# Sparse graph attention on one core: sums of products on DVE for more tiles, an earlier request of h, and record loads from another queue

## The chip, the cores and the metric

The kernel runs on one core of a Trainium2 chip. The metric is the device time of the program in microseconds; lower is better. A core has these engines: TensorE (PE, with its weight load PEld), VectorE (DVE), ScalarE (ACT), GpSimd (POOL) and SyncE (SP). Each runs its own instructions in a fixed order, and they wait for one another through semaphores. DMAs are issued by SP, ACT and POOL; those of one engine stand in that engine's order like its other instructions.

## The reference

One layer of graph attention with a residual, for 4096 nodes with 512 features, 8 heads of 64. Cut to what matters:

```python
hs = layer_norm(x, ln1_scale, ln1_bias)           # sources
ht = layer_norm(h_target, ln1_scale, ln1_bias)    # targets
q = (ht @ Wq + bq).reshape(T, H, HD) / sqrt(HD)
k = (hs @ Wk + bk).reshape(S, H, HD)
v = (hs @ Wv + bv).reshape(S, H, HD)
logits = einsum('thd,shd->hts', q, k)
logits = where(adj[None] != 0, logits, -1e30)
ctx = einsum('hts,shd->thd', softmax(logits), v).reshape(T, D)
ht = layer_norm(ht + ctx @ Wo + bo, ln2_scale, ln2_bias)
x = _layernorm(x + ht + gelu(ht @ W1) @ W2)
```

`adj` is 4096 x 4096 and sparse: each entry is set with probability 0.00195, then mirrored, and the diagonal is set, so a target has some 17 sources. All masks are ones. W1 is 512 x 2048, W2 is 2048 x 512. All is float32.

## The kernel before

The kernel has a sparse path, which is the one that runs here, and a dense one behind a flag. The sparse path has these stages.

1. **Projections and lists** (to about 300 us). k and v of all 4096 sources are computed and stored as rows of 1024 numbers in the DRAM table `kvd`. At the same time the rows of `adj` are loaded, and for each target a list of its sources is made; the loads stand in SP's queue. The first 2048 targets are part A, the others part B. In each part the targets are sorted by their number of sources, and a record for each (its count, its own number, its mean and scale for the first norm, its list of sources) is scattered to the table `recs_d`. The lists of part B are made while the first tiles of part A are worked on; the last of them are stored at about 606 us.
2. **Attention**, in 32 tiles of 128 targets. A tile has a fixed number of slots, as many as its longest list may have. In the order of work the tiles, counted from 0, have 11, 13, 14, 15, 15, 16, 17, 17, 18, 19, 19, 20, 22, 23, 24, 39 slots (part A, `NA` = 16 tiles), then 12, 38, 13, 24, 14, 23, 15, 22, 15, 20, 16, 19, 17, 18, 17, 18 (part B). Tile 0 is a group of its own, then tiles 1 and 2, 3 and 4, and so on make groups of two, and tile 31 is one of its own. The ninth tile is tile 8.
3. **Feed-forward** of each group of two tiles (`feed`), woven into the attention of the groups after it.

`_weave` puts attention, feed-forward, the rest of the lists and the loads of weights into one program by costs that are written out in the code. What one engine runs in which order is then settled when the program is built: a scheduling layer orders the instructions of each engine by what they depend on and by the order in which the code issued them. So an instruction that the code issues earlier need not stand earlier on its engine.

**A tile's work.** The record is loaded by `prefetch(i)` (L965 to L979) into one of 7 buffers `rec`; the load of tile i's record therefore waits until the last reader of the record of tile i-7 is done, and that is the scatter of its result to the output (L1281, at the end of `feed`). Tiles 0 and 1 are loaded through POOL's queue, the others through SP's. `front(i)` (L981) then makes q for the tile: POOL gathers the rows of h by the record (`gather`, L964) into a buffer `tq` of 3; ACT normalizes them (L990); PE transposes (L994); ACT scales (L997); PE multiplies by Wq (L1003); DVE adds the bias (L1008). Between these steps stands a `yield`, and every call of `advance` in the attention, two for each slot group, moves each open front one step.

**A slot group** has three slots of a tile (`S` = 3; the last group of a tile may have fewer). For each slot POOL gathers 128 rows of k and v from `kvd`, one for each target (L964, tile `kv`), into a ring of 17 places in part A and 20 in part B. DVE multiplies k by q (L1197) and reduces to logits (L1201). ACT takes exp (L1205 and L1214, and L1178 for the third slot). The weights multiply v: of a full group DVE does the first two slots (L1161) and ACT the third, head by head (`by_scalar`, L1181). PE then transposes the products, four blocks of 128 x 128 a slot, and sums them over the slots of a tile in PSUM (`cps`, L1169). In tiles of part B, DVE first adds the product of the second slot to that of the first (L1165), and PE transposes the sum alone; `values` holds both.

**Order of requests.** `request(k)` asks for slot groups up to four ahead of k in part A and five in part B. `issue(k)`, at the first slot group of tile i, calls `prefetch(i + 2)` and, where tile i has no front yet, starts `front(i)`, so that its gather of h is issued; then it gathers the slots. `finish(i)` is the tail of a tile: it divides by the sum, adds `tq`'s second half (the transposed normalized h, L1092) to the product with Wo (L1096), and so is the last reader of the buffer `tq`; then it takes the second norm.

**The queues around the change.** POOL's queue has all gathers (of kv, h, x), the scatters of results (L1281), the scatters of records (L853) and small powers for the norms (L687). SP's queue has the loads of `adj` (L713), the stores of lists (L766) and the record loads (L978).

Of the kernel before, what the change touches and what calls it, by code (L numbers as in the profile page):

```python
# [17 lines left out]
P = 128  # L18
# [360 lines left out]
RW = E0 + RE  # L379
# [64 lines left out]
def adj_resnorm_kernel(  # L444
# [33 lines left out]
    nc = tc.nc  # L478
# [22 lines left out]
    NA, NBT = len(CAPS_A), len(CAPS_B)  # L501
# [31 lines left out]
    with tc.tile_pool(name="keep", bufs=1) as keep:  # L533
# [17 lines left out]
        with ExitStack() as late:  # L551
# [416 lines left out]
            def prefetch(i):  # L968
                if i >= NT or i in recs:
                    return  # L970
                r0 = TILES[i][0]
                part = 1 if r0 >= PARTS[1][0] * P else 0
                assert part in done
                r0 -= PARTS[part][0] * P
                rec = sp.tile([P, E0 + MAXE], I32, name="rec", bufs=7)

                eng = nc.gpsimd if i < 2 else nc.sync
                eng.dma_start(rec[:, :RW], recs_d[part][r0:r0 + P, :])  # L978
                recs[i] = rec  # L979

            def front(i):  # L981


                rec = recs[i]
                tq = sp.tile([P, 2 * D], F32, name="tq", bufs=3)
                t = tq[:, :D]
                gather(t, h_target, rec[:, TGT:TGT + 1])
                yield
                m = rec[:, RST:RST + 2].bitcast(F32)
                nc.scalar.activation(t, t, AF.Identity, bias=m[:, 1:2], scale=m[:, 0:1])  # L990
                yield
                pt = ps.tile([P, KC, P], F32, name="t", bufs=2)
                for kc in range(KC):
                    nc.tensor.transpose(pt[:, kc, :], t[:, kc * P:(kc + 1) * P], ident)  # L994
                hT = tq[:, D:].rearrange("p (c t) -> p c t", c=KC)
                for kc in range(KC):
                    nc.scalar.activation(hT[:, kc, :], pt[:, kc, :], AF.Identity,  # L997
                                         bias=b1r[:, kc:kc + 1], scale=s1c[:, kc:kc + 1])
                yield
                yield  # L1000
                pq = ps.tile([P, D], F32, name="t", bufs=2)
                for kc in range(KC):
                    nc.tensor.matmul(pq, hT[:, kc, :], wq[:, kc, :], start=kc == 0,  # L1003
                                     stop=kc == KC - 1)
                yield
                yield
                yield
                nc.vector.scalar_tensor_tensor(tq[:, :D], pq, HD ** -0.5, bqr,  # L1008
                                               op0=ALU.mult, op1=ALU.add)
                tqs[i] = tq  # L1010


            SG = [(i, j0, min(S, cap - j0)) for i, (_, cap) in enumerate(TILES)
                  for j0 in range(0, cap, S)]
# [2 lines left out]
            for i, _, n in SG:  # L1017
                if place[-1] + n > RING[i >= NA]:
                    place[-1] = 0
                place.append(place[-1] + n)  # L1020
            first_b = next(k for k, (i, _, _) in enumerate(SG) if i >= NA)
            issued = [0]

            def step(gens, i):

                if i in gens and next(gens[i], StopIteration) is StopIteration:
                    del gens[i]

            def request(k):
# [3 lines left out]
                while issued[0] <= min(k + ahead, len(SG) - 1):  # L1033
# [3 lines left out]
                        assert not mine & set(range(place[m], place[m] + SG[m][2]))  # L1037
                    issued[0] += 1

            def issue(k):  # L1040

                i, j0, n = SG[k]
                if j0 == 0:
                    prefetch(i + 2)
                    if i not in tqs:
                        fronts[i] = front(i)
                        step(fronts, i)
                    if TILES[i][1] > RE:
                        rests[i] = rest_of(i)
                        next(rests[i])  # L1050
                elif j0 + n > 12 and i in rests:
                    for _ in rests.pop(i):
                        pass
                kvs[k] = ring[:, place[k]:place[k] + n, :]
                for j in range(n):
                    gather(kvs[k][:, j, :], kvd[0:N + 1, :], recs[i][:, E0 + j0 + j:E0 + j0 + j + 1])

            def finish(i, p, cps, group, hs, mv):


                rec, tq, cap = recs[i], tqs.pop(i), TILES[i][1]

                nc.vector.scalar_tensor_tensor(p[:, :cap, :], rec[:, E0:E0 + cap].unsqueeze(2)
                                               .to_broadcast([P, cap, H]), 0.0, p[:, :cap, :],
                                               op0=ALU.is_gt, op1=ALU.mult)
                nc.vector.tensor_reduce(sums[:, i, :], p[:, :cap, :].rearrange("p j h -> p h j"),
                                        AX.X, ALU.add)
                ri = sp.tile([P, H], F32, name="ri")
                nc.vector.tensor_scalar_max(ri, sums[:, i, :], SUM_LO)
                nc.vector.reciprocal(ri, ri)  # L1070
                rx = sp.tile([P, KC, P], F32, name="rb", bufs=1)
                rxf = rx.rearrange("p c t -> p (c t)")
                nc.scalar.copy(rxf.rearrange("p (h d) -> p h d", h=H),
                               ri.unsqueeze(2).to_broadcast([P, H, HD]))
                yield
                yield
                prx = ps.tile([P, KC, P], F32, name="t", bufs=2)
                for c in range(KC):
                    nc.tensor.transpose(prx[:, c, :], rxf[:, c * P:(c + 1) * P], ident)
                ct = sp.tile([P, KC, P], F32, name="rb", bufs=1)  # L1080
                nc.scalar.copy(ct, prx)
                yield
                yield
                nc.vector.tensor_mul(ct, cps, ct)
                yield
                yield
                yield
                yield
                pa = ps.tile([P, D], F32, name="t", bufs=2)

                for c in range(KC):
                    nc.tensor.matmul(pa[:, c * P:(c + 1) * P], tq[:, D + c * P:D + (c + 1) * P],  # L1092
                                     ident, is_transpose=True, start=c == 0, stop=False,
                                     skip_group_check=True)
                for c in range(KC):
                    nc.tensor.matmul(pa, ct[:, c, :], wo[:, c, :], start=False,  # L1096
                                     stop=c == KC - 1, skip_group_check=True)
                yield
                h = sp.tile([P, D], F32, name="h")
                nc.scalar.copy(h, pa)  # L1100
                yield
                stats(sp, h, mv[:, len(hs), :], "n2")
                hs.append(h)
                if len(hs) < len(group):
                    return
                nh = len(hs)
                ve = shifted(sp, mv[:, :nh, :], nh, "n2")
                yield
                rs = power(sp, mv[:, :nh, :], nh, "n2", ve)
                yield  # L1110
                nm = negmean(sp, mv[:, :nh, :], rs, nh, "n2")
                for j, h in enumerate(hs):
                    nc.scalar.activation(h, h, AF.Identity, bias=nm[:, j:j + 1], scale=rs[:, j:j + 1])
                yield
                yield
                w = len(hs) * P
                h2T = sp.tile([P, KC, 2 * P], F32, name="h2T")
                for k2 in range(KC // 2):
                    pt = ps.tile([P, 2, 2 * P], F32, name="t", bufs=2)
                    for k in range(2):  # L1120
                        for j, h in enumerate(hs):
                            nc.tensor.transpose(pt[:, k, j * P:(j + 1) * P],
                                                h[:, (k2 * 2 + k) * P:(k2 * 2 + k + 1) * P], ident)
                    for k in range(2):
                        kc = k2 * 2 + k
                        nc.scalar.activation(h2T[:, kc, :w], pt[:, k, :w], AF.Identity,
                                             bias=b2c[:, kc:kc + 1], scale=s2c[:, kc:kc + 1])
                h2Ts[GROUPS.index(group)] = h2T
# [15 lines left out]
            def attention():  # L1144
# [10 lines left out]
                def values(i, j0, n, kv, p, cps, after):  # L1155
# [5 lines left out]
                    nc.vector.tensor_tensor(v4, v4, p[:, j0:j0 + m, :].unsqueeze(3)  # L1161
                                            .to_broadcast([P, m, H, HD]), ALU.mult)
                    slots = list(range(n))
                    if m > 1 and i >= NA:
                        nc.vector.tensor_add(kv[:, 0, D:], kv[:, 0, D:], kv[:, 1, D:])  # L1165
                        slots.remove(1)
                    for j in slots:
# [17 lines left out]
                k = 0  # L1185
# [170 lines left out]
                for g in gens:  # L1356
                    yield from g

            EARLY = 2
            WAIT = 40.0  # L1360
            AHEAD = 4
            UNIT = 60.0
# [102 lines left out]
```

## Time and profile before

| | us |
|---|---|
| median of 4 runs | 1864.02 |
| lowest and highest of them | 1860.98 and 1871.27 |
| the profiled execution | 1860.27 |
| its span, from first to last instruction | 1858.5 |
| granted clock of TensorE, mean | 0.957 |

The costliest groups around the change, with columns line, engine, operation, tiles, shape and count, then the busy time, the mean of one in ns, and the engine's idle time before them with what ended it:

```profile
L964 POOL DMA_INDIRECT kv<-kvd,rec x603 | 757.2, 1256 | 391.4 <-PE cps L1169 154.6 <-issue 134.3 <-DVE kv L1165 55.7
L1169 PE MATMUL cps<-ident,kv 128*128 128x128 f32 x2008 | 265.6, 281 | 48.3 <-DMA kv<-kvd,rec 26.1 <-DVE kv L1161 19.9 <-DVE kv L1165 2.0
L1161 DVE TENSOR_TENSOR kv<-kv,p 128x1024 f32<-128x1024 f32 x202 | 245.6, 1219 | 21.0 <-ACT p L1205 8.3 <-ACT p L1214 7.2 <-issue 3.3
L1165 DVE TENSOR_TENSOR kv<-kv 128x512 f32<-128x512 f32 x101 | 68.8, 686 | 0.3
L990 ACT ACTIVATE tq<-tq,rec 128x512 f32<-128x512 f32 x32 | 26.0, 813 | 112.8 <-DMA tq<-in_L_gnn_h_target_dram,rec 112.4 <-issue 0.4
```

The 603 slots make 2412 transposes; 101 adds save four each, which leaves the 2008 of the second row. Matmuls are pipelined, so the mean of one in the table is longer than the distance between two starts.

### The profile page before, as it was taken

To read this page: it belongs to the slowest core of one execution; us is meant where nothing else is said; L and a number is where in the kernel's file an instruction comes from. 1 tells how busy PE (TensorE), PEld (TensorE's weight loads), DVE (VectorE), ACT (ScalarE), POOL (GpSimd) and SP (SyncE) were. 2 spreads that over 40 slices of the span, in tenths; PEclk is the share of its full clock that TensorE was granted. 3 is DMA by queue.
4 is the path that set the end of the run, shared out by engine and by line. 5 is a ranking of instruction groups with operands and counts; after the bars stand their busy time and mean duration, and the time that the engine had idled before them with its cause. 6 is when DMAs were issued, how large, how long until landed. Compare 5 with 4: busy or idle time off the path is not lost. (4 is left out here: it accounts for less than half of the span.)

```text
span 1858.5 us, 22978 instructions
## 1 busy us (share of the span) xinstructions
PE 1691.9 (91%) x7030; PEld 1105.1 (59%) x7030; DVE 1429.4 (77%) x2596; ACT 1211.3 (65%) x3111; POOL 970.1 (52%) x804
## 2 busy tenths in 40 slices
PE   7989874698989989999998988899999999999995
PEld 3444432475656656767676656566666666656663
DVE  6999855999989838777968998888978798878000
ACT  5767634577877637676767877676868677766211
POOL 1000143846645577657568777776567676652101
PEclk9999987798989999999999999899999999999998
DMA  9999959988877648767778888778777777763000
GB/s 351 366 380 372 344 167 345 340 282 317 285 277 240 207 119 308 259 229 264 251 263 308 279 286 289 236 265 265 225 249 236 241 258 232 251 219 115 23 0 25
DMA packets 147757, 463.28 MB, mean 249 GB/s; under 512 B 24468, under 2 KB 29160, under 8 KB 147624
## 3 DMA queue, kind: packets, MB, share of 16 engines
q0 software_dynamic: 95696, 342.19, 54.2%
q1 hardware_dynamic: 44112, 96.44, 14.6%
q10 hardware_dynamic: 7816, 23.08, 3.2%
q8 instruction: 58, 0.95, 0.2%
q14 instruction: 75, 0.61, 0.1%
HBM read 430.76 MB, written 30.89 MB: 248 GB/s over the span
## 5 line engine op out<-in xcount | busy, mean ns | idle before, releaser
L964 POOL DMA_INDIRECT kv<-kvd,rec x603 | 757.2, 1256 | 391.4 <-PE cps L1169 154.6
L1313 PE MATMUL po<-w,gt 128*128 128x512 f32 x1024 | 468.0, 600 | 7.8 <-ACT gt L1307 7.8
L1304 PE MATMUL pf<-h2T,w 128*128 128x256 f32 (+1 forms) x2176 | 469.4, 370 | 0.0
L1197 DVE TENSOR_TENSOR kv<-kv,tq 128x1536 f32<-128x1536 f32 (+2 forms) x211 | 352.6, 1678 | 111.2 <-DMA kv<-kvd,rec 99.9
L1304 PEld LDWEIGHTS pf<-h2T,w 128*128 128x128 f32 x2176 | 392.2, 192 | 67.0 <-issue 21.8
L1181 ACT ACTIVATE kv<-kv,pa 128x64 f32<-128x64 f32 x1520 | 391.4, 336 | 4.5
L1201 DVE TENSOR_REDUCE lg<-kv 128x24 f32<-128x1536 f32 (+2 forms) x211 | 350.9, 1670 | 6.8 <-ACT pa L1178 5.7
L1313 PEld LDWEIGHTS po<-w,gt 128*128 128x128 f32 x1024 | 189.8, 193 | 205.3 <-issue 196.2
L1169 PE MATMUL cps<-ident,kv 128*128 128x128 f32 x2008 | 265.6, 281 | 48.3 <-DMA kv<-kvd,rec 26.1
L1169 PEld LDWEIGHTS cps<-ident,kv 128*128 128x128 f32 x2008 | 240.8, 146 | 114.8 <-DVE kv L1161 53.5
L1161 DVE TENSOR_TENSOR kv<-kv,p 128x1024 f32<-128x1024 f32 (+1 forms) x211 | 251.4, 1196 | 21.6 <-ACT p L1205 8.8
L687 POOL TENSOR_TENSOR n_rs<-n_ve,mhalf 128x2 f32<-128x2 f32 (+2 forms) x51 | 54.9, 1077 | 356.1 <-DVE n_ve L680 158.8
L728 ACT ACTIVATE kv<-kv 128x1024 uint8<-128x1024 int32 x128 | 134.7, 1053 | 79.6 <-DMA kv<-in_adj_dram 37.4
L1307 ACT ACTIVATE gt<-pf 128x512 f32<-128x512 f32 x128 | 76.3, 596 | 94.0 <-PE pf L1304 88.5
L929 PE MATMUL pq<-wk,h2T 128*128 128x512 f32 x256 | 126.3, 637 | 12.3 <-ACT h2T L914 6.4
L735 DVE MAX8 cand<-kv 128x8 uint16<-128x103 uint16 (+1 forms) x640 | 131.6, 259 | 0.5
L1003 PE MATMUL t<-wq,tq 128*128 128x512 f32 x256 | 119.5, 609 | 10.8 <-ACT tq L997 10.8
L1307 ACT ACT_TABLE_LOAD x99 | 127.0, 1283 | 1.6
L1205 ACT ACTIVATE p<-lg 128x24 f32<-128x24 f32 (+2 forms) x179 | 39.1, 218 | 133.8 <-DVE lg L1201 83.8
L929 PE MATMUL pq<-wv,h2T 128*128 128x512 f32 x256 | 115.3, 593 | 1.0 <-ACT tq L931 1.0
L1096 PE MATMUL t<-wo,rb 128*128 128x512 f32 x256 | 116.1, 595 | 0.0
L990 ACT ACTIVATE tq<-tq,rec 128x512 f32<-128x512 f32 x32 | 26.0, 813 | 112.8 <-DMA tq<-in_L_gnn_h_target_dram,rec 112.4
(156 smaller groups left out, 1582.9 us busy)
## 6 DMA issues: line engine op xcount, KB each, us to landing
kv<-in_adj_dram SPq DMA_DIRECT2D x128, 512.0 KB
kvd<-tq ACTq DMA_DIRECT2D x24, 512.0 KB
kv<-kvd,rec POOLq DMA_INDIRECT x603
kv<-in_L_gnn_h_target_dram SPq DMA_DIRECT2D x32, 256.0 KB
kv<-in_x_dram SPq DMA_DIRECT2D x15, 512.0 KB
rest_d<-gid SPq DMA_DIRECT2D x32, 160.0 KB
w<-in_L_gnn_W_dram SPq DMA_DIRECT2D x4, 1024.0 KB
kvd<-kv ACTq DMA_DIRECT2D x8, 512.0 KB
```

What stands on the lines that cost most here:

```text
L728: nc.scalar.activation(sg, a, AF.Sign, accum_out=dpart[:, i, h:h + 1])
L735: nc.vector.max(cand[:, h * SQ + s, :], wd[:, w0:w1])
L929: nc.tensor.matmul(pkv, hT[:, kc, j * P:(j + 1) * P], w[:, kc, :], start=kc == 0, stop=kc == KC - 1)
L964: nc.gpsimd.indirect_dma_start(out=dst, out_offset=None, in_=table[:, :], in_offset=bass.IndirectOffsetOnAxis(ap=idx, axis=0))
L1161: nc.vector.tensor_tensor(v4, v4, p[:, j0:j0 + m, :].unsqueeze(3) .to_broadcast([P, m, H, HD]), ALU.mult)
L1169: nc.tensor.matmul(cps[:, c, :], kv[:, j, D + c * P:D + (c + 1) * P], ident, is_transpose=True, start=j0 + j == 0 and c == 0, stop=j0 + n ...
L1181: nc.scalar.mul(v, v, pa[:, hd:hd + 1])
L1197: nc.vector.tensor_tensor(kv[:, :n, :D], kv[:, :n, :D], tq[:, :D].unsqueeze(1).to_broadcast([P, n, D]), ALU.mult)
L1201: nc.vector.tensor_reduce(lg[:, :n, :], kv[:, :n, :D].rearrange("p j (h d) -> p j h d", h=H), AX.X, ALU.add)
L1304: nc.tensor.matmul(pf[:, k, :], w1[(f0 + k) // KC][:, kc, (f0 + k) % KC * P:((f0 + k) % KC + 1) * P], h2T[:, kc, :w], start=kc == 0, stop= ...
L1307: nc.scalar.activation(gt, pf, AF.Gelu_apprx_tanh)
L1313: nc.tensor.matmul(po[j], gt[:, k, j * P:(j + 1) * P], w2[(f0 + k) // KC][:, (f0 + k) % KC, :], start=False, stop=f0 + k == FC - 1, skip_g ...
```

## The change

Three things change.

- `values` adds the second product to the first on DVE for tiles from `NA - 8` on, that is from the ninth tile (tile 8), where before it was from tile 16. Tiles 8 to 15 have 61 slot groups with at least two products of DVE.
- A front may begin when the slot group one or two ahead of the one being issued is the first of its tile, if the tile three before it has had its last transposes of `tq` issued (`turned`). It gathers its rows of h at once and then waits through empty steps, two for each slot group of lead, and two more for tiles after tile 16.
- All record loads are issued from POOL's queue.

```diff
-                eng = nc.gpsimd if i < 2 else nc.sync
-                eng.dma_start(rec[:, :RW], recs_d[part][r0:r0 + P, :])
+                nc.gpsimd.dma_start(rec[:, :RW], recs_d[part][r0:r0 + P, :])
                 recs[i] = rec
 
-            def front(i):
+            def front(i, idle=0):
 ...
                 gather(t, h_target, rec[:, TGT:TGT + 1])
-                yield
+                for _ in range(1 + idle):
+                    yield
                 m = rec[:, RST:RST + 2].bitcast(F32)
...
+            begun_fronts, turned = set(range(EARLY)), set()
...
+            def begin(i, lead):
+
+                if i not in begun_fronts:
+                    begun_fronts.add(i)
+                    fronts[i] = front(i, 2 * lead + (2 if i > NA else 0))
+                    step(fronts, i)
+
             def issue(k):
 
+                for d in (1, 2):
+                    if k + d < len(SG) and SG[k + d][1] == 0 and SG[k + d][0] - 3 in turned:
+                        begin(SG[k + d][0], d)
                 i, j0, n = SG[k]
                 if j0 == 0:
                     prefetch(i + 2)
-                    if i not in tqs:
-                        fronts[i] = front(i)
-                        step(fronts, i)
+                    begin(i, 0)
...
                     nc.tensor.matmul(pa, ct[:, c, :], wo[:, c, :], start=False,
                                      stop=c == KC - 1, skip_group_check=True)
+                turned.add(i)
                 yield
...
                     slots = list(range(n))
-                    if m > 1 and i >= NA:
+                    if m > 1 and i >= NA - 8:
                         nc.vector.tensor_add(kv[:, 0, D:], kv[:, 0, D:], kv[:, 1, D:])
                         slots.remove(1)
```

## Prediction

> **What bounds the kernel now.** The chain of waits comes first on the page and says nothing here: it holds seven pieces, from 1840 us on. So the next views are the page's busy shares and the table of stages: I cut the span where the first multiply of q and k (L1197) of each new group of tiles starts.
>
> ```profile
> PE 1691.9 (91%) x7030; PEld 1105.1 (59%) x7030; DVE 1429.4 (77%) x2596; ACT 1211.3 (65%) x3111; POOL 970.1 (52%) x804
> ```
> ```profile
> 653.90:766.40 112.50, 105.26 (x474) 72.00 (x473) 67.42 (x71) 64.61 (x175) 75.67 (x68) 0.97 0.66 222
> 766.40:858.00 91.60, 91.60 (x434) 64.64 (x433) 71.96 (x71) 66.27 (x182) 54.23 (x49) 1.00 0.71 241
> 858.00:950.00 92.00, 89.02 (x430) 63.26 (x429) 81.09 (x83) 70.34 (x201) 58.61 (x50) 1.00 0.77 263
> 950.00:1054.40 104.40, 97.91 (x461) 69.33 (x461) 86.06 (x80) 73.46 (x205) 81.01 (x66) 0.97 0.87 304
> 1054.40:1159.60 105.20, 93.67 (x412) 64.84 (x411) 95.49 (x98) 77.08 (x228) 82.27 (x60) 0.97 0.83 278
> 1159.60:1246.20 86.60, 77.97 (x328) 52.73 (x327) 74.45 (x84) 62.58 (x170) 64.99 (x48) 0.94 0.75 249
> ```
>
> The columns are length, then busy time of PE, PEld, DVE, ACT, POOL, then granted clock, share of DMA and GB/s. The rows are tiles 9 and 10, 11 and 12, 13 and 14, 15 and 16, 17 and 18, 19 and 20. From 653.9 on, PE is busy nearly all the time: its order is fixed, so the end is PE's work plus PE's idle time plus what half clock costs. DVE follows close behind: 81.1 of 92.0 in tiles 13 and 14, where it still makes no sums of products, and 95.5 of 105.2 (0.908) in tiles 17 and 18, where it does.
>
> Third, the waits, for why PE stands in these stages:
>
> ```profile
> ACT tq L990 <- DMA tq<-in_L_gnn_h_target_dram,rec: 112.4, 26, 12.1
> DVE kv L1197 <- DMA kv<-kvd,rec: 99.9, 36, 12.8
> PE t L994 <- ACT tq L990: 21.6, 4, 8.6
> ```
> ```profile
> SPq L978 <- DMA out_dram<-xt,rec: 911.2, 22, 129.2
> ```
>
> ACT stands 112.4 us for the gathered rows of h, and in four places PE stands behind it. The record loads stand 911 us in SP's queue until the output scatter seven tiles earlier has landed and freed their buffer. The timeline around tile 18 shows one such place, a table of stretches what follows it:
>
> ```profile
> 1110.17 0.97 POOL L964 DMA_INDIRECT tq<-in_L_gnn_h_target_dram,rec  x1 [0.30 <-issue]
> 1115.35 0.81 ACT L990 ACTIVATE tq<-tq,rec 128x512 f32<-128x512 f32 x1 [4.23 <-DMA tq<-in_L_gnn_h_target_dram,rec]
> 1116.22 1.12 PE L994 MATMUL t<-ident,tq 128*128 128x128 f32 x4 [4.96 <-ACT tq L990]
> ```
> ```profile
> 1116.10:1119.50 3.40, 3.28 (x14) 3.19 (x15) 1.32 (x3) 3.34 (x10) 2.60 (x3) 0.50 0.75 197
> 1143.40:1146.80 3.40, 3.40 (x11) 2.83 (x12) 3.39 (x4) 3.34 (x9) 2.79 (x3) 0.50 0.96 345
> 1191.20:1201.40 10.20, 3.96 (x12) 3.30 (x13) 3.12 (x3) 4.54 (x16) 7.76 (x9) 0.50 0.78 263
> ```
>
> After each of the gaps of 4.96 (tile 18), 3.71 (19) and 8.62 us (20) the granted clock is 0.50 for 3.4, 3.4 and 10.2 us; half of that is lost too.
>
> **The change, part by part.**
>
> *The sums.* Tiles 8 to 15 have 61 slot groups with two products that DVE weighed (6, 6, 6, 7, 7, 8, 8, 13). Each gets an add and loses four transposes. In the timeline 12 transposes take 1.47 us and 8 take 1.04, so PE saves 0.43 us each, 26.2 in all. DVE pays 0.686 by its row (L1165, 101 of them); where the next instruction stands ready it starts 0.60 later (1110.45, then 1111.05), so 0.60 to 0.686, 36.6 to 41.8 in all. Whether the saving comes through is settled stage by stage. Lower end: PE alone sets the length. Upper end: DVE's new busy time at the share 0.908 of tiles 17 and 18, the nearest stage that has the adds.
> - Tile 8: -2.6 (6 x 0.43; DVE has 81.1 of the 91.4 us from 562.5 and PE 86.0).
> - Tiles 9, 10: 12 x 0.43 = -5.2; DVE has 67.4 of 112.5, so it covers the adds.
> - Tiles 11, 12: -6.0 by PE (14 adds); DVE 72.0 + 8.4 to 9.6, over 0.908, is 88.5 to 89.9, so -2 to -3. I take -4.
> - Tiles 13, 14: -6.9 by PE (16 adds); DVE 81.1 + 9.6 to 11.0 is 100 to 101 of 92, so up to +9. DVE's free 10.9 us are just filled. I take +3.
> - Tiles 15, 16: -5.6 by PE (13 adds, all in tile 15); DVE 86.1 + 7.8 to 8.9 is 103 to 105 of 104.4, so 0. I take -2.
>
> Together -10.8, between -26 and +2.
>
> *Rows of h sooner.* In the instruction order of the two built programs the gather is sooner only in places, because it needs its record. Counted in kv gathers ahead of it in GpSimd's queue: tile 18 from 352 to 341, tile 19 from 365 to 361; tiles 20 to 31 move by 3 at most; tiles 10, 12, 14 stand later (145 to 150, 184 to 186, 225 to 229). ACT's scaling (L990) stays within one exponential of its old place nearly everywhere, as the added empty steps make it; tile 18's comes three sooner. Tile 18: 11 gathers at about 1.25 us apart are 13.8 us, more than ACT's wait of 4.23: PE's gap of 4.96 and 1.7 of half clock go. Tile 19: 5.0 us sooner against a wait of 7.41, of which PE saw 3.71: that gap and 1.7 go as well. At most -12.1, at least 0; I take -11. Tile 20's gather hangs on its record and that on a scatter (1184.69, record 1188.68, gather 1193.16), so its 8.62 + 5.1 stay; but PE has 12 more FFN products ahead of L994 at that place, which brings the scatter nearer: I take -3, between -13.7 and +3. Others: 0, between -5 and +5. The buffer that the gather now takes sooner is free: the condition on `turned` asks that tile i-3's last transposes already stand in the program.
>
> *Record loads on GpSimd.* 30 loads leave SP and join the queue of the gathers. On SP little hangs behind them: of the loads of adjacency the last is issued at 564.6 us, the last store of a list at 605.6, and before that only tile 7's record held two of them up, by 5.5 us. A load there took 0.585 us (two at the start) and 0.3 to the next, so 0.9; the 25 from tile 7 on cost 22 us of GpSimd. They also wait there for the scatter to land. In tile 12's place that wait exists already, put down to the x gather: scatters at 759.66 and 760.98, 2.79 us idle, gather of x at 764.76, of h at 767.31. The new order (scatter twice, record, x, record, x, h, kv) makes h and all kv behind it 1.8 us later per pair. PE felt 21.6 of ACT's 112.4, a fifth: 12 pairs x 1.8 x 0.19 = +4. For kv gathers held up (queued behind: DVE's next L1197, already waiting 99.9) I take +3. Together +7, between 0 (the ring covers them) and +22.
>
> The Trainium skill, "SBUF — State Buffer", section "Who interferes with whom", speaks against this part: a DMA issued by GpSimd is starved while DVE holds the port they share, and one from SP isn't, though it lists tensor_tensor among the operations seen not to stall DMAs. The trace shows a mean of 1.256 us against 0.94 for an undisturbed gather, and single ones of 4.12 us, so the issues do get longer; by the page's pair of 0.62 us alone and 3.1 under a DVE copy (section "A bandwidth-pool intuition that's wrong (but worth ruling out)") an estimate is 30 x 2.5 = 75 us more on GpSimd, which by the fifth makes the sum 14 us worse. I keep my rows.
>
> *Order of ACT.* The built program holds 212 table loads instead of 200; at 1.283 us that is 15.4 us on ACT, which is 65% busy. DVE waits 15.5 us in all for ACT's p, so I take +2, between 0 and +15.
>
> **Sum:** -10.8 - 11 - 3 + 7 + 2 = -15.8. The profiled execution took 1860.27 us (span 1858.5): it becomes 1844.5, the span 1842.7. The median of the four runs is 3.75 above the profiled one, so 1848.
>
> **The rivals.**
>
> *DVE becomes the bound (slower).* If DVE's waits in tiles 11 to 16 are latencies that don't shrink, the 43 adds there land in full: 43 x 0.686 = +29.5. With tiles 8 to 10 at -7.8, tiles 18 and 19 at -11, +9 for loads and tables: +20, 1884. It decides from where DVE's free 10.9 us in tiles 13 and 14 are used up, that is at the 16 adds. For: 81 of 92 busy. Against: PE at 100% in tiles 11 and 12, and GpSimd waiting 20.1 us there for transposes (L1169), so much of DVE's waiting is PE's. Chance 0.20.
>
> *It doesn't do what it says (no change).* The rows of h come no sooner where it counts, since their records don't; tiles 18 and 19 get other waits. -10.8 + 9 = -2: 1862. For: the gather's place for tiles 10, 12, 14, 20. Against: 11 gathers of lead for tile 18. Chance 0.19.
>
> *PE alone counts (much faster).* All 26.2 come through, the 21.6 before L994 go, and half of the three stretches and of one more of 3.4 us (10.2): -58 + 9 = -49, 1815. For: PE's share. Against: DVE's share with the adds. Chance 0.15.
>
> **How the numbers follow.** The forecast has 0.46, with a range of its own of 1834 to 1860 from the bounds of the stages and the loads. A measurement of this kernel can tell about 0.5% (9.3 us) from no change. Faster than 1854.7: 0.40 of the forecast, the 0.15, and 0.03 of the second rival: 0.58. Within: 0.22. Slower: 0.20. Eight in ten lie between 1822, which leaves out the greater part of the third rival, and 1876, which leaves out about half of the first.
>
> **What would show it.** 1764 transposes at L1169's place, 162 adds; PE in tiles 9 to 12 shorter by about 9 us; in tiles 13 and 14 DVE above 90 us and PE with new gaps; no gap before L994 of tiles 18 and 19, but one for tile 20; GpSimd standing for scatters ahead of record loads. I am wrong if tiles 13 to 16 together grow by over 10 us, if the waits for h stay at some 110 us with PE behind them, or if waits for kv gathers grow past 130 us.

## The result and the profile after

The changed kernel takes 1862.24 us in the median of 42 runs, the kernel before 1863.73 us in 63 runs: a ratio of 0.9993, with a 95% interval of 0.9984 to 1.0003. No change can be told. The profiled execution has a span of 1860.5 us (before 1858.5).

The page's busy shares of the kernel after, and three of its groups (busy time, mean of one in ns | idle time before them and what ended it):

```profile
PE 1677.2 (90%) x6786; PEld 1079.5 (58%) x6786; DVE 1460.6 (79%) x2657; ACT 1226.9 (66%) x3123; POOL 1017.4 (55%) x834
...
L1181 PE MATMUL cps<-ident,kv 128*128 128x128 f32 x1764 | 243.7, 285 | 82.0 <-DVE kv L1177 37.8
...
L990 ACT ACTIVATE tq<-tq,rec 128x512 f32<-128x512 f32 x32 | 26.0, 814 | 157.0 <-DMA tq<-in_L_gnn_h_target_dram,rec 150.8
...
L1177 DVE TENSOR_TENSOR kv<-kv 128x512 f32<-128x512 f32 x162 | 110.8, 686 | 0.3
```

The change does what it says: 1764 transposes, 162 adds, 30 more instructions on POOL. PE is busy 14.7 us less than before and yet the span doesn't shrink: PE's idle time, summed over its gaps, grew from 140.6 to 164.6 us. The table of stretches, cut as before:

```profile
657.40:767.60 110.20, 98.92 (x413) 65.17 (x412) 74.14 (x83) 65.67 (x176) 82.09 (x69) 0.97 0.71 228
767.60:862.20 94.60, 88.44 (x378) 60.22 (x378) 79.90 (x84) 67.89 (x183) 61.51 (x51) 0.96 0.74 243
862.20:957.70 95.50, 88.81 (x373) 59.59 (x372) 85.73 (x85) 70.25 (x198) 67.70 (x52) 0.95 0.77 247
957.70:1061.10 103.40, 95.18 (x423) 64.70 (x422) 95.78 (x104) 78.67 (x225) 84.72 (x64) 0.98 0.82 275
1061.10:1169.70 108.60, 97.82 (x415) 64.24 (x414) 96.08 (x103) 78.85 (x217) 88.43 (x67) 0.94 0.86 290
1169.70:1256.70 87.00, 76.01 (x321) 51.37 (x320) 73.56 (x82) 62.33 (x169) 63.37 (x51) 0.94 0.77 261
```

In tiles 11 and 12 (second row) PE was busy without a break; now it has 88.44 of 94.60 us, at a lower clock (0.96 where it was 1.00). The waits say for what (total, times, longest):

```profile
PE cps L1181 <- DVE kv L1177: 37.8, 17, 8.2
...
DVE kv L1173 <- ACT p L1217: 36.1, 17, 7.5
...
POOL rec L977 <- DMA out_dram<-xt,rec: 25.3, 11, 3.8
...
PE t L994 <- ACT tq L990: 7.2, 2, 5.9
```

PE stands 37.8 us for sums (2.0 before; 23.4 of the 37.8 lie in tiles 8 to 15, up to 1055 us, the rest in tiles that had their sums before), GpSimd 25.3 us for scatters ahead of record loads, and PE's 21.6 us behind the normalized rows of h have fallen to 7.2, although ACT's own wait for these rows went up, from 112.4 to 150.8 us. Something was won and something was lost; the experiments part the two.

### The profile page after: what moved, and what is told of

It reads as the page before. It is cut to its first block, busy times and chain, and to the rows that moved or that the text cites. A ratio compares the mean times of both kernels' runs of the same rounds, so it can differ in the third digit from the quotient of the medians.

```text
span 1860.5 us, 22452 instructions
## 1 busy us (share of the span) xinstructions
PE 1677.2 (90%) x6786; PEld 1079.5 (58%) x6786; DVE 1460.6 (79%) x2657; ACT 1226.9 (66%) x3123; POOL 1017.4 (55%) x834
## 5 line engine op out<-in xcount | busy, mean ns | idle before, releaser
L964 POOL DMA_INDIRECT kv<-kvd,rec x603 | 775.2, 1286 | 378.6 <-PE cps L1181 145.2
L1325 PE MATMUL po<-w,gt 128*128 128x512 f32 x1024 | 473.3, 604 | 11.9 <-ACT gt L1319 10.1
L1181 PE MATMUL cps<-ident,kv 128*128 128x128 f32 x1764 | 243.7, 285 | 82.0 <-DVE kv L1177 37.8
L1181 PEld LDWEIGHTS cps<-ident,kv 128*128 128x128 f32 x1764 | 214.0, 147 | 158.5 <-issue 68.5
L1173 DVE TENSOR_TENSOR kv<-kv,p 128x1024 f32<-128x1024 f32 (+1 forms) x211 | 252.2, 1197 | 51.2 <-ACT p L1217 36.1
L687 POOL TENSOR_TENSOR n_rs<-n_ve,mhalf 128x2 f32<-128x2 f32 (+2 forms) x51 | 50.8, 996 | 331.0 <-DVE n_ve L680 147.1
L990 ACT ACTIVATE tq<-tq,rec 128x512 f32<-128x512 f32 x32 | 26.0, 814 | 157.0 <-DMA tq<-in_L_gnn_h_target_dram,rec 150.8
L1177 DVE TENSOR_TENSOR kv<-kv 128x512 f32<-128x512 f32 x162 | 110.8, 686 | 0.3
```

Source lines behind the costliest of these rows:

```text
L964: nc.gpsimd.indirect_dma_start(out=dst, out_offset=None, in_=table[:, :], in_offset=bass.IndirectOffsetOnAxis(ap=idx, axis=0))
L1181: nc.tensor.matmul(cps[:, c, :], kv[:, j, D + c * P:D + (c + 1) * P], ident, is_transpose=True, start=j0 + j == 0 and c == 0, stop=j0 + n ...
L1325: nc.tensor.matmul(po[j], gt[:, k, j * P:(j + 1) * P], w2[(f0 + k) // KC][:, (f0 + k) % KC, :], start=False, stop=f0 + k == FC - 1, skip_g ...
```

## The experiments

Each kernel was timed together with the kernel before; ratios of kernels that were not timed together compare less well. 0.1% is 1.9 us. "Half clock" below is the time in which the granted clock was 0.50 and PE was busy; half of it is lost.

### The parts, alone and together

```diff
# adds alone (kernel before with this)
-                    if m > 1 and i >= NA:
+                    if m > 1 and i >= NA - 8:
# record loads alone
-                eng = nc.gpsimd if i < 2 else nc.sync
-                eng.dma_start(rec[:, :RW], ...)
+                nc.gpsimd.dma_start(rec[:, :RW], ...)
# fronts alone: `begin`, `turned` and `idle` of the change, the other two parts as before
# adds and fronts: the change, with the record loads as before
```

The adds alone:

> The kernel before with the adds from tile 8 on, alone. Record theory (the adds pay, and the record loads on GpSimd give it back by making the rows of h later): 8 to 12 us faster, waits of ACT for h near 112 us. DVE theory (what PE saves, DVE pays): 0 to +10 us, with PE waiting over 20 us for the add.

The fronts alone:

> The kernel before with the earlier fronts alone, records from SP. Record theory: waits of ACT for h fall below 100 us, 3 to 11 us faster. If the gather hangs on its record anyway: waits near 112 us and no change within 3 us.

The record loads alone:

> The kernel before with the record loads on GpSimd alone. Record theory: waits of ACT for h rise to some 140 to 160 us, 5 to 12 us slower. DVE theory: no change within 3 us, since PE and DVE have the same work.

Adds and fronts together:

> The changed kernel with the record loads back on SP. Record theory: waits of ACT for h below 112 us, 10 to 18 us faster than before. DVE theory: within 4 us of the changed kernel's time.

| kernel | median, us (before 1860.04) | ratio, 95% interval |
|---|---|---|
| adds alone | 1868.31 | 1.0066 (1.0039 to 1.0092) |
| fronts alone | 1845.66 | 0.9920 (0.9895 to 0.9946) |
| record loads alone | 1870.80 | 1.0064 (1.0039 to 1.0088) |
| adds and fronts | 1847.97 | 0.9949 (0.9930 to 0.9968) |

In us of 1860 that is +12 for the adds, -15 for the fronts, +12 for the record loads. They don't simply add: given the fronts, the adds cost 5 (0.9920 to 0.9949), and given both, the loads cost 8 (0.9949 to 0.9993, this last pair not timed together). One part gains, two lose, and what is left is nothing. The waits that the record theory named did not come: ACT's waits for h are 111.0 us with the fronts (below 100 expected), 126.8 with the record loads (140 to 160) and 120.0 with adds and fronts (below 112). The gain of the fronts, larger than the 3 to 11 us expected, is not in these waits.

### Why the adds lose

Two kernels that leave a piece out or double it. In the first, tiles 8 to 15 neither add nor transpose the second product, so it is missing from their results: PE's saving without DVE's work. In the second, DVE adds but PE still transposes all slots, so that product counts twice: DVE's work without PE's saving.

```diff
# saving alone
                     if m > 1 and i >= NA:
                         nc.vector.tensor_add(kv[:, 0, D:], kv[:, 0, D:], kv[:, 1, D:])
                         slots.remove(1)
+                    elif m > 1 and i >= NA - 8:
+                        slots.remove(1)
# add alone: the elif holds the tensor_add instead of the remove
```

> The kernel before, but in tiles 8 to 15 the second product is neither added nor transposed: it is left out of the sum, so PE has 244 transposes less and DVE nothing more. If PE sets the pace of these tiles: 20 to 28 us faster than before, and the adds' loss (e1_adds, 1.0066) is all DVE's. If the length of these stages is set by a chain over several engines: under 10 us faster, with PE's saved time coming back as its idle time.

1841.64 us (before 1862.42), 0.9885 (0.9838 to 0.9932).

> The kernel before, with DVE's add in tiles 8 to 15 but all transposes kept, so that the second product counts twice: DVE has 61 adds more and PE saves nothing. If DVE has room there: within 8 us of before. If DVE's adds lie on the path: 25 to 40 us slower. Together with e5_skip the two should add up to e1_adds, some +12 us, if the parts are independent.

1870.80 us, 1.0040 (1.0015 to 1.0065).

So the saving is worth 21 us where nothing waits for a sum, near the 26.2 that PE makes less. With the add it is gone, and the add's own price doesn't explain it: -21 and +7 would make -14, and the adds alone measured +12. The halves are not independent; the loss arises where PE, with less to do, comes to a sum that isn't there. The profiled executions give the account; transposes left out are -26.2 us as the prediction worked them out, the other columns are differences to the kernel before (idle time 140.6, half clock 83.4 us):

| kernel | work of PE | idle of PE | half clock, halved | sum | span, measured |
|---|---|---|---|---|---|
| saving alone | -26.2 | +3.8 | +2.6 | -19.8 | -18.6 |
| add alone | 0 | +8.6 | +5.0 | +13.6 | +13.6 |
| adds (both) | -26.2 | +18.7 | +7.8 | +0.3 | +3.4 |
| the whole change | -26.2 | +24.0 | +6.9 | +4.7 | +2.0 |

In the whole change PE's last instruction also lies 7.5 us nearer to the end of the span, which the sum leaves out. What else the sums miss is mostly in the first column: PE's work (its busy time less half of the half clock) fell by 25.2, 22.9 and 21.5 us in the three kernels with fewer transposes. With the adds alone all that PE saves is spent on standing and on the clock behind it. PE's waits in that kernel:

```profile
PE cps L1169 <- DVE kv L1161: 40.2, 9, 25.2
PE cps L1169 <- DVE kv L1165: 25.1, 13, 4.6
```

The second row was 2.0 us, once, before; 17.9 of its 25.1 us, in ten places, lie in tiles 8 to 15. And one such place in its timeline (start, length, then engine, line, operation; the idle time before it in brackets):

```profile
729.40 1.22 DVE L1161 TENSOR_TENSOR kv<-kv,p 128x1024 f32<-128x1024 f32 x1
...
730.54 1.74 DVE L1201 TENSOR_REDUCE lg<-kv 128x24 f32<-128x1536 f32 x1
...
732.20 0.68 DVE L1165 TENSOR_TENSOR kv<-kv 128x512 f32<-128x512 f32 x1
...
732.94 1.97 PE L1169 MATMUL cps<-ident,kv 128*128 128x128 f32 x8 [4.60 <-DVE kv L1165]
...
733.15 3.94 POOL L964 DMA_INDIRECT kv<-kvd,rec  x1 [5.36 <-DVE kv L1165]
```

The products are done at 730.62. The add doesn't follow at once: it needs its product, so the builder put another instruction of DVE between, a reduce for the next slot group (1.74 us). The sum is there at 732.88. PE stands 4.60 us, of which the last 2.3 are the add and what stands before it, and its next eight transposes take 1.97 us where eight took 1.04. GpSimd's gather for the ring waits for the same sum. Over all adds up to 1058 us of this trace the sum ends 2.08 us after its product in the mean, and in 60 of 64 cases another instruction stands between. The prediction paid 0.6 to 0.69 us per add and asked whether DVE has room; what PE pays is this latency, and it pays it where DVE has room too. Of the 17.9 us of standing, 14.8 come after the product is done, so that the sum alone is late; in the other 3.2 the product is late itself. The latency costs only where PE follows closely: 45 of the 61 sums were there over 0.3 us before PE came. In tiles 16 to 31 of the kernel before, the sums come as late after their products (some 2 us in the mean), but PE comes 14.1 us after the sum in the mean and stands 2.0 us in all. In tiles 12 to 15 it comes 8.3 us after a full group's product in the kernel before and 5.1 us after it with the adds.

Does the place matter? Adds in tiles 8 to 11 alone (`i >= NA or NA - 8 <= i < NA - 4`), then in tiles 12 to 15 alone (`i >= NA - 4`):

> The kernel before with the adds in tiles 8 to 11 only (25 of the 61 slot groups). Measured for all 61 alone: a ratio of 1.0066, 8 to 12 us slower. Theory A (the cost is PE standing for the sum at the head of a group's transposes, with half clock after it; it arises wherever DVE is late, whatever its share of busy time): a part of the loss is here, 1.001 to 1.005. Theory B (the prediction's: DVE has room in these tiles and the saving comes through): 25 x 0.43 = 10.8 us faster, 0.994 to 0.997.

1865.41 us (before 1862.35), 1.0026 (1.0006 to 1.0045).

> The kernel before with the adds in tiles 12 to 15 only (36 of the 61). Theory A (PE standing for the sum): the other part of the loss, 1.001 to 1.006. Theory B (the prediction's: DVE's room is just used up): 0.998 to 1.002. Rival C (DVE's time is the bound there, the first rival of the prediction): 36 x 0.686 = 25 us slower, 1.010 to 1.014, with DVE over 95% busy in tiles 13 to 16.

1864.11 us, 1.0015 (0.9999 to 1.0031).

Both ratios lie where the theory of PE's standing put them. In tiles 8 to 11, where DVE has the most room, 11 us of gain don't come. DVE as the bound of whole stages is refuted: in tiles 13 to 16 it is busy 85.88 of 91.19 and 95.73 of 102.75 us, at most 94%, and the 25 us are not there. (The second result alone would also fit the prediction.) In the first of the two PE stands 16.7 us for sums, in four places; three of them, of 4.27, 4.62 and 5.67 us, lie in tiles 9 to 11 (window 562 to 1055 us):

```profile
PE cps L1169 <- DVE kv L1165: 14.6, 3, 5.7
```

Of these 14.6 us, 8.5 come after the product is done; ahead of the longest, DVE itself had stood 5.48 us for ACT's p before it made that product.

Does it help to give PE something to do meanwhile? In tiles 8 to 15 the third slot's product, ACT's, is transposed first and the sum last:

```diff
                         slots.remove(1)
+                        if i < NA:
+                            slots.reverse()
...
-                                             is_transpose=True, start=j0 + j == 0 and c == 0,
+                                             is_transpose=True, start=j0 == 0 and j == slots[0] and c == 0,
```

> The kernel before with the adds in tiles 8 to 15, and there the product of the third slot (ACT's) is transposed first and the sum last, so that PE has four transposes to make while DVE adds. Theory A (the loss is PE's standing for the sum): PE's idle time put down to the add falls from 25 us (with the sum first) below 12 and the loss goes, 0.994 to 1.002. Rival C (DVE's 42 us of added work are the cost, wherever PE stands): 1.005 to 1.009 as with the sum first. If ACT's product is late instead, the wait moves to it and the time stays.

1865.54 us (before 1862.35), 1.0018 (1.0001 to 1.0036). PE's waits from 562 to 1055 us, first of the adds with the sum first, then with the sum last:

```profile
PE cps L1169 <- DVE kv L1165: 17.9, 10, 4.6
...
PE cps L1169 <- ACT kv L1181: 2.9, 1, 2.9
```
```profile
PE cps L1171 <- DVE kv L1165: 10.9, 8, 2.6
...
PE cps L1171 <- ACT kv L1183: 5.4, 4, 3.5
```

The loss is smaller than the 1.0066 with the sum first (the intervals don't touch, but the two were not timed together), and it lies below the band that DVE's added work as such was given. Of the 18 us of standing 7 went, and 2.5 came to ACT's product; over the whole span the waits for sums are 19.5 us, not below 12 as expected, and PE's idle time in all, 162.8 us, is no less than with the sum first (159.3), in a profiled execution that was the slowest of its 12. The time speaks for PE's standing as the cause, the trace only weakly, and no order of a group's transposes tried here lets the saving arrive.

### Where the gain of the fronts comes from

The fronts have two edits: the sooner request, and the two empty steps more for tiles from 17 on.

```diff
# steps alone: the fronts' part with no request ahead
-                for d in (1, 2):
+                for d in ():
# request alone: the fronts' part without the two steps
-                    fronts[i] = front(i, 2 * lead + (2 if i > NA else 0))
+                    fronts[i] = front(i, 2 * lead)
```

> The sooner request of h taken away again, and only the two empty steps that fronts of tiles 17 to 31 make before ACT scales the rows kept; record loads on SP, no adds in tiles 8 to 15. Theory A (the gain of 14 us comes from the later place of the scaling and the transposes in ACT's and PE's order, so that work that is ready stands ahead of those that wait for h): most of it is here, 1846 to 1852, and PE has no gap before the transposes of h in tiles 17 to 20. Theory B (it comes from gathers that start sooner): little, 1858 to 1864, and the gaps stay.

1842.83 us (before 1860.83), 0.9909 (0.9877 to 0.9941).

> The sooner request of h with its two empty steps for each slot group of lead, so that the scaling keeps its place, but without the two further steps of tiles 17 to 31; record loads on SP, no adds in tiles 8 to 15. Theory A (the later place does it): little, 1857 to 1863, PE's gaps before the transposes of h stay. Theory B (sooner gathers do it): 1846 to 1852, ACT's waits for h well below 112 us.

1863.59 us, 1.0012 (0.9989 to 1.0035).

The whole gain is in the steps. PE's waits from 1055 to 1330 us, first with the steps alone, then with the request alone:

```profile
PE cps L1182 <- DVE kv L1178: 8.0, 4, 4.0
PE t L1004 <- ACT tq L998: 5.7, 3, 4.4
PE t L1091 <- ACT rb L1085: 0.6, 1, 0.6
```
```profile
PE t L995 <- ACT tq L991: 15.7, 2, 11.1
PE t L1135 <- ACT h L1126: 2.8, 2, 2.4
```

With the steps, PE doesn't stand for the transposes of h there at all; with the request, it stands 15.7 us (L995 and L991 are L994 and L990 of before). ACT's waits tell that this is not because the rows come sooner, again steps, then request:

```profile
ACT tq L991 <- DMA tq<-in_L_gnn_h_target_dram,rec: 132.1, 25, 12.7
```
```profile
ACT tq L991 <- DMA tq<-in_L_gnn_h_target_dram,rec: 108.2, 22, 11.9
```

ACT waits longer with the steps, and theirs is the faster kernel. What the steps moved is PE's place: counted in the trace, the transposes of h of tiles 17 to 31 stand behind 8 more transposes of products (tile 19: none) and 8 to 24 more feed-forward products than before, while with the request alone they stand exactly where they stood. Work that is ready now runs while ACT waits. The steps also moved one gather: tile 18's stands behind 332 kv gathers instead of 352 (347 with the request alone), so that for tile 18's gap, 4.96 of the 17.3 us, the two causes aren't parted. The account for the steps alone: idle time of PE -15.2, half clock +4.0, of which half, sum -13.2; span -12.8.

Is a later place good everywhere? The steps were given to all tiles from 2 on (`2 if i >= EARLY else 0`), in kernels with the table described next: without and with the sooner request.

> The table of the targets' numbers and no sooner request, as in the run before, with the two empty steps in the fronts of all tiles from 2 on instead of from 17 on; record loads on SP, no adds in tiles 8 to 15. If the later place of the scaling and the transposes is what gains wherever PE stands for h, tile 8's gap (4.3 to 5.8 us and the half clock after it) goes too: 3 to 6 us below 1845, a ratio of 0.988 to 0.991. If q then comes late for a tile's first multiply, DVE gets new waits for it in tiles 2 to 16: 0.994 to 1.000.

1851.22 us (before 1856.98), 0.9964 (0.9944 to 0.9983). The expected gain is a miss: with the steps only from tile 17 on, the same kernel has 0.9924 (not timed together). The run can't show what the steps gain at tile 8's gap, because with the table and the steps from 17 on PE no longer stands for the rows of h there; it shows what they cost where there is no gap. The waits of DVE:

```profile
DVE tq L1012 <- PE t L1007: 58.6, 11, 10.6
...
DVE kv L1177 <- ACT p L1221: 46.4, 21, 5.8
```

They were 45.1 and 23.0 us with the steps from 17 on. q now comes late in the first tiles: tiles 3 to 6 take 179.8 us instead of 170.2, tile 8 takes 49.7 instead of 42.5.

> The same with the sooner request of h. Sent with the run without it, so that the two are compared on one chip: if the sooner request gives nothing, both lie within 0.2% of each other; if it helps once records are early (0.988 against 0.992 in separate calls), this one is 0.3 to 0.5% lower.

1846.86 us, 0.9942 (0.9923 to 0.9962). With the request it is 0.2% lower, and the intervals overlap.

### Why the record loads lose

If the cost is that GpSimd stands for the scatter which frees a record's buffer, it goes when no scatter reads the record. So the targets' numbers were kept in a table of their own, read by the gather of x and the output scatter; a record's last reader is then its own tile's attention.

```diff
+        tgts = keep.tile([P, NT, 1], I32, name="tgts")
...
+                nc.sync.dma_start(tgts[:, me, :], recs_d[part]...[:, :, TGT:TGT + 1])
...
-                rec = sp.tile([P, E0 + MAXE], I32, name="rec", bufs=7)
+                rec = sp.tile([P, E0 + MAXE], I32, name="rec", bufs=6)
...
-                            ap=recs[i][:, TGT:TGT + 1], axis=0),
+                            ap=tgts[:, TILES[i][0] // P, :], axis=0),
...
-                            gather(xt, x, recs[i][:, TGT:TGT + 1])
+                            gather(xt, x, tgts[:, TILES[i][0] // P, :])
```

In the kernel before:

> The kernel before, with the targets' numbers for the gather of x and the output scatter loaded once into a table of their own, and 6 record buffers in place of 7: a record's buffer is free when the attention of its tile ends, not when its result is stored. Record theory (the late record is what holds the gather of h): the record loads' waits for the scatter (911 us) go, waits of ACT for h fall from 112 to under 60 us, 8 to 20 us faster. If the gather's place in GpSimd's order is what holds it: waits stay above 90 us, no change within 4 us.

1848.14 us (before 1862.42), 0.9931 (0.9901 to 0.9962). The time is as the record theory had it, the wait isn't: ACT's waits for h fall to 86.8 us, not under 60.

In the changed kernel, record loads on GpSimd:

> The changed kernel with the same table and 6 record buffers, record loads still on GpSimd. If their harm (e3_recpool, 1.0064) is the wait for the scatter in GpSimd's queue: 10 to 14 us faster than the changed kernel, as e4_adds_early. If it is their 0.9 us of GpSimd each: under 4 us faster than the changed kernel.

1843.01 us, 0.9880 (0.9843 to 0.9916).

In the changed kernel, with the record loads back on SP:

> The changed kernel with the table of the targets' numbers (no record buffer waits for an output scatter) and with record loads back on SP. Against the kernel without the adds in tiles 8 to 15 (sent with it) it prices those adds where no record is late; against the changed kernel with the table and loads on GpSimd (0.988, 1843 us) it prices the bare issue of 30 loads there. Theory A (the record loads cost through waiting in GpSimd's queue for a scatter, the adds some 2 us as with record loads late): within 3 us of 1843, and 2 to 4 us above the kernel without the adds. Theory B (GpSimd's time for the issues counts, 30 x 0.9 = 27 us of which a third is felt): 1832 to 1837. If the adds cost their full 8 us, it lies 8 above the kernel without them.

1842.43 us (before 1860.83), 0.9903 (0.9869 to 0.9937).

With the buffers free, loads on GpSimd cost nothing that can be seen (0.9880 and 0.9903, not timed together). So the price hangs on the late buffers and isn't the bare issue of the loads. In the changed kernel the table is worth 1.1% (0.9993 to 0.9880), in the kernel before 0.7%: late records cost it too, and more where they are loaded from GpSimd.

GpSimd doesn't stand longer for scatters, though. In the kernel before it stood for them ahead of the gather of x; with the loads alone on GpSimd the same wait comes ahead of the loads, and in the changed kernel with the table it is back ahead of x, while the loads stay on GpSimd and the cost is gone. The three, in this order:

```profile
POOL xt L964 <- DMA out_dram<-xt,rec: 23.2, 13, 4.5
```
```profile
POOL rec L977 <- DMA out_dram<-xt,rec: 19.4, 11, 4.4
...
POOL xt L964 <- DMA out_dram<-xt,rec: 2.3, 3, 0.8
```
```profile
POOL xt L967 <- DMA out_dram<-xt,tgts: 23.4, 14, 2.8
```

What changes is the order behind the scatter. With the loads alone on GpSimd, the gather of h of the even tiles 18 to 30 starts later after the scatter than before, by 0.8 to 2.8 us in six of the seven and by 13.8 us for tile 20; the median is 1.9 us. How this becomes 8 to 12 us is not shown. GpSimd's timeline in the changed kernel at tile 24 (start, length, then as above):

```profile
1354.59 0.99 POOL L1293 DMA_INDIRECT out_dram<-xt,rec  x1 [0.30 <-issue]
1357.87 0.58 POOL L977 DMA_DIRECT2D rec<-rec  x1 [2.29 <-DMA out_dram<-xt,rec]
1358.76 2.24 POOL L964 DMA_INDIRECT xt<-in_x_dram,rec  x1 [0.31 <-issue]
1361.00 0.59 POOL L977 DMA_DIRECT2D rec<-rec  x1
1361.89 3.56 POOL L964 DMA_INDIRECT xt<-in_x_dram,rec  x1 [0.30 <-issue]
1365.75 0.94 POOL L964 DMA_INDIRECT kv<-kvd,rec  x1 [0.30 <-issue]
1367.00 0.94 POOL L964 DMA_INDIRECT kv<-kvd,rec  x1 [0.31 <-issue]
1368.25 1.21 POOL L964 DMA_INDIRECT tq<-in_L_gnn_h_target_dram,rec  x1 [0.30 <-issue]
```

GpSimd stands 2.29 us for the scatter; two record loads, two gathers of x and two of kv then run before the gather of h, which leaves 10.4 us after the record load was issued (5.0 in the kernel before). ACT stands 8.12 us for its rows (L990 at 1372.37); at this tile it was 2.05 before.

### The fastest kernel

Fronts and table, record loads on SP, no adds in tiles 8 to 15; and the same without the sooner request.

> The kernel before with the sooner request of h and, besides, the targets' numbers kept in a table of their own (loaded once for each part of the targets after its sort), so that the gather of x and the output scatter no longer read the record, and a record's buffer is free as soon as its tile's own work is done; record loads on SP, no adds in tiles 8 to 15. Alone, the sooner request came to a ratio of 0.992 (14 us) and the freed records to 0.993 (14 us). Theory A (the two remove different waits, the one PE's standing for h and DVE's for kv, the other the scatter ahead of a record): the gains add, 1830 to 1838 us. Theory B (both remove the same wait, that for h): no more than the better of the two, 1844 to 1850.

1838.74 us (before 1860.83), 0.9884 (0.9851 to 0.9916).

> The two empty steps of tiles 17 to 31 alone (no sooner request) with the table of the targets' numbers, record loads on SP, no adds in tiles 8 to 15: the sooner request taken away from the fastest kernel so far (0.9884). If the sooner request gives nothing, as the two runs that part it from the empty steps say, 0.986 to 0.991; if it helps once records are early, 0.992 to 0.995.

1845.11 us (before 1862.35), 0.9924 (0.9897 to 0.9951).

The fastest beats the kernel before by 1.2%, and so the changed one, whose own ratio is 0.9993. The gains of the fronts (0.8%) and of the table (0.7%) add up only in part. With the table alone in the kernel before, none of the waits of PE for the normalized rows of h is left (21.6 us before), so the steps find little to save: without the request they give no more than the table alone (0.9924 against 0.9931, not timed together). What the sooner request is worth where records are early stays open: 0.4% between these two, not timed together, and 0.2% in the pair above, each time with intervals that overlap. Against the kernel with the adds (0.9903, timed together) the fastest is 3.7 us ahead by the medians, within what the intervals leave open.

## Why the prediction was wrong

It forecast a clear gain, 1848 us, and there is none. The time lies in the range, close to its second rival's 1862, but not for that rival's reason: the part it called idle does gain.

- **The step that failed** is the sums, -10.8 us; they cost 12 alone and 5 beside the fronts. The prediction settled the question by busy shares: where DVE is busy 67.4 of 112.5 us, "it covers the adds", and PE's saving comes through. In tiles 9 and 10 -5.2 was forecast; alone the adds made them 2.3 us longer. A busy share says whether an engine has time for the work, not when the result is there. The sum lies between a product and the transposes that PE has next in its fixed order, and it comes 2.08 us later there; PE, with less to do, runs up to it and stands. The upper end, +2 (the stages' own ends add up to about -1), was too low for the same reason: both ends looked at throughput alone.
- **DVE as the bound**, the first rival, was wrong as well. The stretches of tiles 13 to 16 grew by 2.5 us together, not 10, and DVE is busy 85.73 of 95.50 us in tiles 13 and 14, not above 90.
- **Rows of h sooner**, -14 in all: right in size (-15 for the fronts), wrong in cause. The working gave the gain to 11 gathers of lead for tile 18 and 4 for tile 19. The request alone, which gives tiles 18 and 19 five and four, changes nothing. The prediction saw the "12 more FFN products ahead of L994" and used them for tile 20 alone, for -3; such work ahead of the transposes was what gained. It also passed over tiles 16 and 17, whose gathers of h stand 27 and 15 kv gathers later in the changed kernel (296 after 269, 308 after 293). ACT's waits for these rows lay at 106 to 151 us in every kernel whose records wait for scatters, the fast and the slow; what changed is whether PE stood behind them.
- **Record loads**, +7: in its bounds of 0 to 22, with +12 alone and +8 beside the rest, so the term was somewhat too small. The working had h 1.8 us later per pair of tiles and the wait for the scatter there before; the 1.9 us and the 23.2 us above agree. How PE comes to lose 8 to 12 us by it stays open. The estimate of 75 us more for issues, from the Trainium skill's page "SBUF — State Buffer", section "A bandwidth-pool intuition that's wrong (but worth ruling out)", isn't borne out: a record load on GpSimd takes 0.581 us in the changed kernel (32 of them, 18.6 us), as the two at the start did before.
- **ACT's table loads**, +2: not measured apart. They are there (105 under the line of gelu instead of 99), and ACT's p came later for DVE: 36.1 us in the row shown, where its two rows were 8.3 and 7.2 before.
- Of the signs named, 1764 transposes, 162 adds, no gap before L994 of tiles 18 and 19 and GpSimd's standing came true. Tile 20's gap, which was to stay, went too. PE's busy time in tiles 9 to 12 did fall, by 9.5 us (98.92 and 88.44 after 105.26 and 91.60), and the stretches together still grew by 0.7.

## What to carry to other kernels

An operation that saves the bound engine work but stands between its operands and it must be priced by when its result is there (its own time and that of whatever the issuing engine's order puts before it) and by how closely the bound engine follows. Where an engine stands for data that are late, look first at its order: a waiting step moved behind work that is ready was worth 15 us here, and the same data asked for sooner nothing. A DMA that must wait belongs in a queue in which nothing urgent stands behind it, or what it waits for has to go: freeing the buffers took away the cost of the loads on GpSimd.

## What the runs showed of the hardware

Short standings cost PE twice. With the adds alone its idle time grew by 18.7 us and its busy time at half clock by 15.6. A gap of 3.83 us at 673.7 and one of 4.60 at 728.3 were followed by 10.2 and 6.8 us at a granted clock of 0.50. "TensorE: Matmul & The Clock Gate" of the Trainium skill, section "HAM oscillation — how this bites in real kernels", draws the line for such gaps at some 3.4 us. The traces agree only roughly: a gap of 3.21 us at 778.0 in the same kernel and one of 2.09 at 1622.1 in the kernel before were followed by 3.4 us of half clock too, and one of 3.98 at 1663.6 in the kernel before by none. What had not been expected is how much of a saving can go that way: 7.8 of 26.2 us.
